# The MLP's last hidden tile with upper part, lower part and ones in one: two matrix products in place of three

## The chip, the cores and the metric

The kernel runs on one core of a Trainium2 chip. The metric is the device time of one execution in microseconds (us), the median of several runs. A core has TensorE (PE, matrix products into PSUM), VectorE (DVE), ScalarE (ACT), GpSimd (POOL) and the queue SP, which here issues every DMA.

## The reference

Two branches work on the layer-normed input `xn` of 4 x 1024 tokens of width 256: full attention with 16 heads of width 16, and two layers of windowed attention, each followed by an MLP. The output is `x + s * silu(g)`, with `s` from the first branch and `g` from the second. The MLP is the part that is changed:

```python
HID = int(DIM * 4 * 2 / 3)          # 682
h = shift_token(x)
mu = h.mean(-1, keepdims=True)
var = h.var(-1, keepdims=True)
h = (h - mu) / jnp.sqrt(var + 1e-05) * lg + lb
h = h @ w1 + b1
a, g = jnp.split(h, 2, axis=-1)
h = a * jax.nn.gelu(g, approximate=False)
x = x + h @ w2 + b2
```

## The kernel before

**Phases.** The second branch goes through phases: attention of layer 0 (phase 2), MLP of layer 0 (phase 3), attention of layer 1 (phase 4), MLP of layer 1 (phase 5). The 64 heads of the first branch (matrices `mx` and `sc`, exponentials `es`, sums `acc`; projections `pp`, `qa`, `th`) belong to no phase and are spread over the whole time, so that the two branches fill each other's gaps.

**The order** is not written by hand. A recorder takes down every operation with the tiles that it reads and writes. A list scheduler (`lay_out`) then gives each operation a price (`price`), lets each engine take what is due first (`nc.vt`), and so fixes one order for each engine; `put` issues the operations in that order (line 536 of the profile is there, so every operation has that line). Consecutive products into one PSUM bank are joined into pieces of up to 1500 ns of price. Each engine works through its queue in order.

**Precision.** Products with full precision are made from float32r parts: a value is split into an upper part (`split`: ACT copies with rounding) and a lower part (the rest, subtracted on VectorE or POOL), and `mm3` makes three products: upper x upper, upper x lower, lower x upper.

```python
def mm3(out, ah, al, bh, bl, start, stop):
    for k, (l, r) in enumerate(((ah, bh), (ah, bl), (al, bh))):
        nc.tensor.matmul(out, lhsT=l, rhs=r, start=start and k == 0, stop=stop and k == 2)
```

**The MLP** (`mlp_phase`) runs over 8 blocks of 512 tokens. The 682 hidden rows make 5 tiles of 128 rows and a sixth (`kt = 5`) of 42 (`TAIL`). For each block:

- `up` pieces (6 products of 128x512) make the gate half of the hidden rows; ACT adds the bias and puts them into `ge`, then one GELU goes over all six tiles. `ta` keeps the other half of the sixth tile.
- POOL clears rows 32 to 127 of the sixth tile of `ge` before that, and after the GELU sets rows 64 to 95 to 1. Row 64 is then the factor of `b2`, which the host has put into row 64 of the sixth tile of `w2`; the other rows meet zeros.
- VectorE multiplies: the sixth tile from `ta`, the others from PSUM as each `up` piece ends. Each tile is split into `hh` (ACT) and `hl` (POOL, 128x512 each).
- `y`: for each of four groups of 128 tokens, 6 tiles x 3 products of 128x256 into one bank, in pieces of 12 and 6; VectorE adds the residual (`xm`).
- In layer 1 SiLU, the output projection of the other branch (`foT`, `fth`, `ftl`, `fs`) and the last sum (`fx`) follow.

`ge`, `hh` and `hl` have one buffer each, so a block's first cast into `hh` waits until the block before has finished `y`. PSUM: three banks (`psB`) serve `up`, `y`, `dT` and other uses in rotation, two (`psM`) serve `mx` and `pp`, two `sc`, one `acc`.

**Weights.** `load_split` brings `w2` in by two DMAs and splits it into `w2_h` (ACT) and `w2_l` (POOL) at the start of each MLP phase.

Of the kernel before, what the change touches and what calls it, by code (L numbers as in the profile page):

```python
# [10 lines left out]
F32R = mybir.dt.float32r  # L11
# [3 lines left out]
ALU = mybir.AluOpType  # L15
# [4 lines left out]
P = 128  # L20
B, N, D = 4, 1024, 256
# [10 lines left out]
NKT = 6  # L32
TAIL = HID - 5 * P
W1T = 11 * P
BLK = 512
# [512 lines left out]
def f32(ap):  # L548
    return ap.bitcast(F32)
# [30 lines left out]
def fused_kernel(  # L580
# [17 lines left out]
    nc = Recorder(tc)  # L598
# [18 lines left out]
    def bank(name):  # L617
        return psB.tile([P, 512], F32, tag="b", name=name)
# [72 lines left out]
    def split(hi, lo, src, lo_eng=None):  # L691

        nc.scalar.copy(hi, src)
        (lo_eng or nc.vector).tensor_tensor(lo, src, f32(hi), ALU.subtract)
# [5 lines that stand above are left out]
# [219 lines left out]
    def stack(a):  # L919


        j, h = divmod(a, HALF)
        sq, sk = stacks[a % NSTACK]
        nc.vt = of_head(a - AHEAD - 1.0)
        at, m = 3 * DH * h, 3 * DH

        step = N // 2 if a < 2 else N
        for lo in range(0, N, step):
            s = slice(lo, lo + step)
            for g, dst in enumerate((sq, sk)):  # L930
                rows = qk_d[j % 2][g, at : at + m, s]
                three = rows.rearrange("(p s) t -> p s t", s=3)
                nc.sync.dma_start(dst[:m, s], rows)
                nc.sync.dma_start(dst[m : m + 2 * DH, s], three[:, g : g + 2, :])
                last = nc.sync.dma_start(dst[m + 2 * DH : 2 * m, s], three[:, 2 * g, :])
        if a >= NSTACK:
            last = nc.sync.dma_start(sq[96:98, :], sq[100:102, :])
        return last

    def maxima(a):  # L940

        sq, sk = stacks[a % NSTACK]
        nm = a2.tile([P, NC, 2], F32, tag="nm", name=f"nm{a}")
        for c in range(NC):
            nc.vt = of_head(a - AHEAD + c / NC)
            for n in range(2):
                ps = bank_a(f"mx{a}_{c}_{n}")
                nc.tensor.matmul(
                    ps, lhsT=sq[:, c * P : (c + 1) * P], rhs=sk[:, n * 512 : (n + 1) * 512],
                    start=True, stop=True,  # L950
                )
                nc.vector.tensor_reduce(nm[:, c, n : n + 1], ps, AX.X, ALU.max)
        mt = bank_t(f"mT{a}")
        mx = mt[:, 2 * P : 2 * P + NC]
        mp = mps[a % 2]
        nc.vector.tensor_reduce(mx, nm, AX.X, ALU.max, negate=True)
        nc.vector.tensor_copy(top(mp[:, 0, :]), mx)
        nc.vector.tensor_tensor(top(mp[:, 1, :]), mx, mp[:, 0, :], ALU.subtract)
        pt = mt[: 2 * NC, :P]
        nc.tensor.transpose(pt, mp.rearrange("p i c -> p (i c)"), ident)  # L960
        mr = a2.tile([2 * NC, P], BF16, tag="mr", name=f"mr{a}")
        nc.scalar.copy(mr, pt)
        for i in range(2):
            last = nc.sync.dma_start(
                sq[96 + i : 97 + i, :].rearrange("o (c t) -> o c t", t=P),
                mr[i * NC : (i + 1) * NC, :],
            )
        return last
# [63 lines left out]
    for a in range(-NSTACK, TOTAL):  # L1032
        m = a + NSTACK
        if a >= 0:
            attend(a)
        if m < TOTAL:
# [3 lines left out]
            last = stack(m)  # L1040
# [4 lines left out]
            last = maxima(m)  # L1045
# [6 lines left out]
    def load_split(pool, tag, hi, lo, src, name, lo_eng=None):  # L1052

        n = hi.shape[1]
        for i in range(0, n, 1024):
            m = min(1024, n - i)
            st = pool.tile([P, 1024], F32, tag=tag, name=f"{name}_{i}")
            nc.sync.dma_start(st[:, :m], src[:, i : i + m])
            split(hi[:, i : i + m], lo[:, i : i + m], st[:, :m], lo_eng or nc.gpsimd)
# [216 lines left out]
    def mlp_phase(layer):  # L1276
# [5 lines left out]
        p1 = nc.pool(f"m1_{layer}", 1, phase=nc.phase)  # L1282
# [13 lines left out]
        with nc.unit():  # L1296
            for t in range(11):
                m = P if t < 10 else 64 + TAIL
                for half in range(2):
                    nc.tensor.matmul(  # L1300
                        pb[:m, t : t + 1], lhsT=sts[half][:, t * P : t * P + m],
                        rhs=vec[:, 1, half : half + 1], start=(half == 0), stop=(half == 1),
                    )
        nc.vector.tensor_tensor(b1_sb[:, :10], b1_sb[:, :10], pb[:, :10], ALU.add)
        m = 64 + TAIL
# [6 lines left out]
        w2_h = wp.tile([P, NKT * D], F32R, name=f"w2h{layer}")  # L1312
        w2_l = wp.tile([P, NKT * D], F32R, name=f"w2l{layer}")
        load_split(p1, "ge", w2_h, w2_l, w2[layer], f"w2s{layer}")
        if layer == LAYERS - 1:
            wout_h = wp.tile([P, 2 * D], F32R, name="wouth")
            wout_l = wp.tile([P, 2 * D], F32R, name="woutl")
            load_split(p1, "ge", wout_h, wout_l, w_out, "wouts")
# [3 lines left out]
        for at, (b, i) in enumerate(blocks):  # L1322
            n = f"{layer}_{b}_{i}"
# [32 lines left out]
            def up(t):  # L1356
                ps = bank(f"up{n}_{t}")
                m = P if t < 10 else 64 + TAIL
                for half in range(2):
                    w = slice(t * P, t * P + m)  # L1360
                    mm3(ps[:m], w1_h[:, half, w], w1_l[:, half, w], dh[:, half], dl[:, half],
                        half == 0, half == 1)
                return ps
# [6 lines left out]
            ge = p1.tile([P, NKT, BLK], F32, tag="ge", name=f"ge{n}")  # L1370
            nc.gpsimd.memset(ge[32:64, 5, :], 0.0)
            nc.gpsimd.memset(ge[64:, 5, :], 0.0)
            for kt in (5, 0, 1, 2, 3, 4):
                ps = up(5 + kt)
                m, rows = (P, slice(0, P)) if kt < 5 else (TAIL, slice(64, 64 + TAIL))
# [7 lines left out]
            table(gelu)  # L1383
            nc.vt = of_layers(part, (at + 0.4) / len(blocks))
            hh = p1.tile([P, NKT, BLK], F32R, tag="hh", name=f"hh{n}")
            hl = p1.tile([P, NKT, BLK], F32R, tag="hl", name=f"hl{n}")
            for kt in (5, 0, 1, 2, 3, 4):
                m = P if kt < 5 else TAIL
                if kt == 5:

                    nc.gpsimd.memset(ge[64:96, kt, :], 1.0)
                    nc.vector.tensor_tensor(ge[:m, kt, :], ta[:m], ge[:m, kt, :], ALU.mult)
                else:
                    nc.vector.scalar_tensor_tensor(
                        ge[:, kt, :], up(kt), b1_sb[:, kt : kt + 1], ge[:, kt, :],
                        ALU.add, ALU.mult,
                    )
                split(hh[:, kt, :], hl[:, kt, :], ge[:, kt, :], nc.gpsimd)
            nc.vt = of_layers(part, (at + 0.7) / len(blocks))
            for k in range(4):  # L1400
                ps = bank(f"y{n}_{k}")[:, :D]
                for kt in range(NKT):
                    s, w = slice(k * P, (k + 1) * P), slice(kt * D, (kt + 1) * D)
                    mm3(ps, hh[:, kt, s], hl[:, kt, s], w2_h[:, w], w2_l[:, w], kt == 0, kt == NKT - 1)
                nc.vector.tensor_tensor(xr[:, k, :], ps, xr[:, k, :], ALU.add)
            if layer < LAYERS - 1:
                nc.sync.dma_start(
# [10 lines left out]
            for k in range(4):  # L1418
                pt = bank(f"foT{n}_{k}")[:, : 2 * P]
                for half in range(2):  # L1420
                    s = slice(half * P, (half + 1) * P)
# [4 lines left out]
                ps = bank(f"fs{n}_{k}")[:, :D]  # L1426
                for half in range(2):
                    s, w = slice(half * P, (half + 1) * P), slice(half * D, (half + 1) * D)
# [10 lines left out]
    for layer in range(LAYERS):  # L1439
        attention_phase(layer)  # L1440
        mlp_phase(layer)
# [91 lines left out]
```

## Time and profile before

| | |
|---|---|
| median of 3 runs | 2175.7 us (2174.28 to 2176.49) |
| profiled execution | 2178.46 us, its span 2176.7 us |
| mean granted TensorE clock | 0.987 |
| `y` products | 1152 of 128x256, 384 of each of three kinds, 154.8 us busy |
| `hl` splits on POOL | 96, median 1292 ns |
| `hh` casts on ACT | 96, median 620 ns |
| memsets of `ge` on POOL | 48, median 519 ns |
| layer 0's `y` | from 872.0 us |
| layer 1's `y` | to 2165.7 us |

The span runs from the first to the last instruction of the profiled execution; busy times are summed over one engine. Products on PE overlap, so the length of one `y` product (283 ns) is more than the distance to the next. The waits name what an engine stood for last; the chain is the one that ended last, followed back from the end.

### The profile page before, as it was taken

The numbers are of one execution on the slowest core, as the hardware profiler recorded it, in microseconds if no ns is written. First come the engines' busy times: TensorE is split into PE (matmuls) and PEld (weight loads), VectorE is DVE, ScalarE is ACT, GpSimd is POOL, SyncE is SP. The second block draws the span as 40 slices with busy tenths as digits, with TensorE's granted clock in tenths as the row PEclk, the third lists the DMA queues.
The fourth block names the chain that finished last, engine by engine and source line by source line (L and its number), as shares of the span: only waits on it lengthen the run. The fifth ranks groups of instructions, "written<-read, shape, count | busy, mean of one in ns | idle before, by whom it ended". The sixth has DMA issues, their size and how long they took to land.

```text
span 2176.7 us, 46620 instructions
## 1 busy us (share of the span) xinstructions
PE 2085.6 (96%) x16760; PEld 1376.1 (63%) x16760; DVE 1658.9 (76%) x4008; ACT 1604.4 (74%) x3830; POOL 1089.0 (50%) x1369
## 2 busy tenths in 40 slices
PE   4899999999999999999999999999999999999998
PEld 3356656666666645876665556666566665478887
DVE  6899799898888877576558888888888888855433
ACT  4577877788888777566658878778777788676774
POOL 5346755566666632333127556665657555023433
PEclk8799999999999999999999999999999999999999
DMA  4856655565565443231124535454354444503212
GB/s 129 169 118 162 157 129 119 136 153 112 115 126 131 95 109 101 78 83 60 35 84 116 131 77 102 105 126 101 69 112 108 89 90 86 153 11 97 77 50 83
DMA packets 496255, 227.62 MB, mean 105 GB/s; under 512 B 336788, under 2 KB 479264, under 8 KB 496024
## 3 DMA queue, kind: packets, MB, share of 16 engines
q1 hardware_dynamic: 496024, 224.63, 44.5%
q8 instruction: 133, 2.18, 0.4%
q14 instruction: 98, 0.80, 0.1%
HBM read 111.30 MB, written 49.82 MB: 74 GB/s over the span
## 4 chain that ended last, share of the span: by engine, by line
PE 64%; ACT 16%; DVE 9%; DMA 3%; issue 3%; POOL 2%; SPq 1%; ACTq 0%; POOLq 0%; DVEq 0%
PE up L536 11%; PE sc L536 7%; PE acc L536 7%; PE qkv L536 7%; PE mx L536 6%; PE y L536 6%; ACT sm L536 5%; PE po L536 5%; ACT es L536 3%; PE px L536 3%; PE sb L536 3%; DVE rotb L536 2%; DVE nm L536 2%; PE pp L536 2%; ACT ph L536 2%
## 5 line engine op out<-in xcount | busy, mean ns | idle before, releaser
L536 DVE TENSOR_REDUCE nm<-mx 128x1 f32<-128x512 f32 x1024 | 669.0, 682 | 106.2 <-PE mx L536 103.7
L536 ACT ACTIVATE es<-sc 128x512 f32<-128x512 f32 x1024 | 575.5, 600 | 151.3 <-PE sc L536 147.7
L536 PE MATMUL mx<-sk,sq 128*128 128x512 bf16 x1024 | 352.6, 387 | 22.1 <-DVE nm L536 15.6
L536 PE MATMUL sc<-sq,sk 128*128 128x512 bf16 x1024 | 343.7, 384 | 19.2 <-ACT es L536 15.8
L536 POOL TENSOR_TENSOR ph<-sm,ph 128x1024 f16<-128x1024 f32 (+1 forms) x128 | 258.6, 2021 | 177.9 <-ACT ph L536 163.3
L536 PE MATMUL qkv<-wqkvh,ht 128*128 128x512 f32 x768 | 302.0, 435 | 1.9 <-ACT sqv L536 0.5
L536 PE MATMUL acc<-es,v 128*32 128x512 f32 x2048 | 275.0, 609 | 0.3 <-ACT ac L536 0.2
L536 ACT ACTIVATE sm<-sm,nb 128x256 f32<-128x256 f32 (+1 forms) x512 | 247.4, 489 | 4.0
L536 POOL TENSOR_TENSOR qr<-rotb 128x256 f32<-128x256 f32 x256 | 182.9, 734 | 133.9 <-DVE rotb L536 120.3
L536 PEld LDWEIGHTS <-sq 128*128 128x128 bf16 x1024 | 89.9, 99 | 157.0 <-issue 112.3
L536 PEld LDWEIGHTS qkv<-wqkvh,ht 128*128 128x128 f32 x768 | 146.4, 191 | 57.4 <-ACT sqv L536 4.9
L536 PEld LDWEIGHTS <-pht 128*128 128x128 f16 x4800 | 151.5, 98 | 45.3 <-issue 30.2
L536 DVE TENSOR_TENSOR rotb<-qkv,tab 128x1024 f32<-128x1024 f32 x128 | 156.0, 1220 | 25.4 <-PE qkv L536 9.8
L536 PEld LDWEIGHTS <-sk 128*128 128x128 bf16 x1024 | 88.9, 98 | 130.3 <-issue 89.9
L536 POOL TENSOR_TENSOR hl<-ge,hh 128x512 fp32r<-128x512 f32 x96 | 122.2, 1291 | 96.5 <-ACT hh L536 95.5
L536 PE MATMUL po<-vs,pht 128*128 128x64 bf16 x4800 | 161.6, 193 | 2.8 <-DMA pht<-ph 2.2
L536 PE MATMUL qkv<-wqkvl,ht 128*128 128x512 f32 x384 | 152.1, 396 | 0.0
L536 PE MATMUL up<-dh,w1h 128*128 128x512 f32 (+1 forms) x352 | 148.5, 422 | 0.1
L536 POOL TENSOR_TENSOR sqv<-sqv 128x512 f32<-128x512 f32 (+1 forms) x128 | 129.6, 1013 | 37.6 <-ACT sqv L536 36.2
L536 PE MATMUL up<-dh,w1l 128*128 128x512 f32 (+1 forms) x352 | 139.1, 395 | 0.0
L536 PE MATMUL up<-dl,w1h 128*128 128x512 f32 (+1 forms) x352 | 138.8, 394 | 0.0
L536 ACT ACTIVATE sqv<-qkv 128x512 f32<-128x512 f32 x128 | 76.5, 597 | 70.5 <-DVE rotb L536 57.1
(271 smaller groups left out, 4739.1 us busy)
## 6 DMA issues: line engine op xcount, KB each, us to landing
xc<-xt_d SPq DMA_DIRECT2D x56, 256.0 KB
qk<-th SPq DMA_DIRECT2D x128, 96.0 KB
xt_d<-nt SPq DMA_DIRECT2D x32, 256.0 KB
ht<-xt_d SPq DMA_DIRECT2D x64, 128.0 KB
tab<-tab SPq DMA_DIRECT2D x64, 128.0 KB
xa<-xr SPq DMA_DIRECT2D x64, 128.0 KB
ht<-xa SPq DMA_DIRECT2D x32, 256.0 KB
xm<-xa SPq DMA_DIRECT2D x16, 512.0 KB
```

Source lines behind the costliest of these rows:

```text
L536: ins = getattr(getattr(nc, engine), method)(*[take(a) for a in args], **{n: take(a) for n, a in kw.items()})
```

## The change

In the sixth tile, 42 of 128 rows were in use, so upper and lower parts fit into one tile: `hh` holds the upper part in rows 0 to 41, the lower part in rows 64 to 105 and ones in rows 106 to 127. The host repeats the last 42 rows of `w2` from row 64 on and puts `b2` into rows 106 and 107. On the chip, after the split, row 107 of `w2_h` is overwritten with the lower part of `b2` by a one-row DMA, and rows 64 to 127 of the sixth tile of `w2_l` are cleared. One product with `w2_h` then gives upper x upper, lower x upper and both parts of the bias; one with `w2_l` gives upper x lower. `hl` has five tiles. The lower part of the sixth tile is subtracted on VectorE (42x512) instead of on POOL; the memset of `ge` after the GELU goes, and two memsets of `hh` (32x512) come.

```diff
@@ load of w2 in mlp_phase
         load_split(p1, "ge", w2_h, w2_l, w2[layer], f"w2s{layer}")
+
+        last = slice((NKT - 1) * D, NKT * D)
+        nc.sync.dma_start(f32(w2_h)[64 + TAIL + 1 : 64 + TAIL + 2, last], f32(w2_l)[64 + TAIL + 1 : 64 + TAIL + 2, last])
+        nc.gpsimd.memset(f32(w2_l)[64:, last], 0.0)
@@ a block
             hh = p1.tile([P, NKT, BLK], F32R, tag="hh", name=f"hh{n}")
-            hl = p1.tile([P, NKT, BLK], F32R, tag="hl", name=f"hl{n}")
+            hl = p1.tile([P, NKT - 1, BLK], F32R, tag="hl", name=f"hl{n}")
             for kt in (5, 0, 1, 2, 3, 4):
                 m = P if kt < 5 else TAIL
                 if kt == 5:
 
-                    nc.gpsimd.memset(ge[64:96, kt, :], 1.0)
+                    nc.gpsimd.memset(f32(hh)[32:64, kt, :], 0.0)
+                    nc.gpsimd.memset(f32(hh)[96:, kt, :], 1.0)
                     nc.vector.tensor_tensor(ge[:m, kt, :], ta[:m], ge[:m, kt, :], ALU.mult)
+                    nc.scalar.copy(hh[:m, kt, :], ge[:m, kt, :])
+                    nc.vector.tensor_tensor(
+                        hh[64 : 64 + m, kt, :], ge[:m, kt, :], f32(hh)[:m, kt, :], ALU.subtract
+                    )
+                    continue
                 else:
...
             for k in range(4):
                 ps = bank(f"y{n}_{k}")[:, :D]
-                for kt in range(NKT):
-                    s, w = slice(k * P, (k + 1) * P), slice(kt * D, (kt + 1) * D)
-                    mm3(ps, hh[:, kt, s], hl[:, kt, s], w2_h[:, w], w2_l[:, w], kt == 0, kt == NKT - 1)
+                s = slice(k * P, (k + 1) * P)
+                for kt in range(NKT - 1):
+                    w = slice(kt * D, (kt + 1) * D)
+                    mm3(ps, hh[:, kt, s], hl[:, kt, s], w2_h[:, w], w2_l[:, w], kt == 0, False)
+                for w2_x in (w2_h, w2_l):
+                    nc.tensor.matmul(ps, lhsT=hh[:, 5, s], rhs=w2_x[:, last], start=False, stop=w2_x is w2_l)
                 nc.vector.tensor_tensor(xr[:, k, :], ps, xr[:, k, :], ALU.add)
@@ on the host
-    w2[:, 5 * P + 64] = a["L0_ffn_b2"]
+    w2[:, 5 * P + 64 : 5 * P + 64 + TAIL] = a["L0_ffn_w2"][:, 5 * P :]
+    for k in range(2):
+        w2[:, 5 * P + 64 + TAIL + k] = a["L0_ffn_b2"]
```

As `lay_out` sees other prices and dependencies, it also gives every engine a slightly different order within the two MLP phases.

## The prediction

> **What bounds the kernel now.** I read the page first, for the engines' shares and the chain that ended last.
>
> ```profile
> PE 2085.6 (96%) x16760; PEld 1376.1 (63%) x16760; DVE 1658.9 (76%) x4008; ACT 1604.4 (74%) x3830; POOL 1089.0 (50%) x1369
> ...
> PE 64%; ACT 16%; DVE 9%; DMA 3%; issue 3%; POOL 2%; SPq 1%; ACTq 0%; POOLq 0%; DVEq 0%
> PE up L536 11%; PE sc L536 7%; PE acc L536 7%; PE qkv L536 7%; PE mx L536 6%; PE y L536 6%; ACT sm L536 5%; PE po L536 5%; ACT es L536 3%; PE px L536 3%; PE sb L536 3%; DVE rotb L536 2%; DVE nm L536 2%; PE pp L536 2%; ACT ph L536 2%
> ```
>
> TensorE (PE) is busy 96% of the span and makes 64% of the chain; `y`, the product that is changed, makes 6% of it. As busy time is an average over stages, I asked next for the windows of the two MLP phases and of the attention layer between them, for all work and then for `y` alone.
>
> ```profile
> 850.00:1136.00 286.00, 284.92 (x1640) 205.33 (x1639) 169.65 (x373) 178.16 (x286) 88.44 (x101) 1.00 0.21 59
> 1136.00:1905.00 769.00, 746.28 (x6697) 464.41 (x6696) 644.70 (x1544) 605.61 (x1577) 437.46 (x552) 1.00 0.47 106
> 1905.00:2177.00 272.00, 262.76 (x1603) 213.68 (x1601) 121.88 (x297) 183.86 (x266) 97.96 (x109) 0.99 0.21 64
> ```
>
> The columns are length, busy PE, weight loads, DVE, ACT, POOL, granted clock. In the first MLP phase PE idles 1.1 us of 286, in the second 9.2 of 272, at full clock; VectorE, ACT and POOL are at most 68% busy there (weight loads run under the products). What PE is spared in these stages should come off the end, unless a wait takes its place. Then the chain in order of time, for the pace of `y`, and the waits of PE:
>
> ```profile
> 882.82 5.76 PE y L536 x48
> ...
> 2041.64 5.75 PE y L536 x48
> ```
>
> ```profile
> PE y L536 <- POOL hl L536: 0.5, 1, 0.5
> ```
>
> 48 products in 5.75 us are 0.120 us each. (The 0.28 us that the `y` rows show is the length of one that overlaps the next.) The wait says that PE stood for `hl` once, 0.5 us, in the whole execution.
>
> **The change part by part.** *Products removed.* Each of 16 blocks has four groups of 128 tokens; each loses one of 18 products: 16 x 4 = 64. In the changed program's order of instructions `y` from `w2h` and `hl` falls from 384 to 320, and nothing else on PE changes in number. 64 x 0.120 = 7.7 us, in stretches where PE is the bound. What stands next to them changes little: PE's order is the same up to the first MLP phase and between the two; within them heads and MLP pieces swap neighbours.
>
> *POOL.* 16 `hl` splits go (1.29 us each by the `hl` row, 20.6 us) and 16 memsets of `ge` (0.52 us); 32 memsets of `hh` of the same form come. That frees 16 x (1.29 - 0.52) = 12.3 us of an engine that is half idle. PE waited 0.5 us for `hl`, so at most 0.5 us of it can be gained. The removed memset waited for the GELU; the new ones wait until the block before has read `hh`, its last `y`. In the block at 1950 us the GELU ended at 1949.6 and ACT's first `hh` cast stood for `y` until 1952.6, so POOL is released 3 us later. Behind it stand this block's `hl` (whose source waited for the same `y` anyway) and in the first phase some `th` and `qa` for heads that run later. In the second phase POOL is busy 98 of 272 us, so this is hidden. The sixth tile's cast on ACT must follow the memset by 0.52 us; PE has five `up` pieces of 1.4 us (7 us) to do before it needs `hh`. Without that cover it is 16 x 0.52 = 8.3 us. In the last block this cast now stands behind SiLU and its two table loads, ahead of the casts that `hl` wait for: one cast pitch, 0.5 us, near the end, where little is left to hide it. I count 0.5.
>
> *VectorE.* 16 subtractions of 42x512 come in. The nearest row is `ge<-ta,ge`, 42x512 with both inputs in SBUF: 0.68 us, so 10.9 us on an engine that is busy 59% and 45% in these phases. Each waits for the ACT cast, and VectorE's queue stands behind it: evictions of `up`, maxima of the heads. In five blocks of the second phase it is placed after the fourth of five evictions and in two after the third, by when the cast is due by the trace; in four of the eight blocks of the first phase it is placed ahead of the first eviction. Can it be lengthened? Two rows (shortest, median and longest, in ns) say what can happen to such an instruction:
>
> ```profile
> L536 DVE TENSOR_TENSOR tab<-tab,scl x16: 407/422/1397, 39.1 to 1272.0; 128x256 f32<-128x256 f32 x16
> ```
>
> ```profile
> L536 DVE TENSOR_TENSOR ge<-ta,ge x16: 673/682/684, 863.0 to 2140.6; 42x512 f32<-42x512 f32 x16
> ```
>
> `tab<-tab,scl` has both inputs in SBUF, as the new subtraction has; its median is 0.42 us and its longest 1.40. `ge<-ta,ge` never grew, but the POOL instruction beside it was a memset. The subtraction will stand among `hl` splits of 1.29 us. So one costs VectorE from 0.68 to 0.68 + 1.29 = 1.97 us. Does PE see it? An `up` piece takes 1.4 us and three banks are in rotation, so a bank may be evicted 2 x 1.4 = 2.8 us after its piece has ended; 1.97 + 0.75 for the eviction itself is 2.72. That is just covered, so I take nothing for it, nearest to the waits of PE on VectorE in the second phase (1.5 us in all); its other end is the first rival. The Trainium skill (SBUF — State Buffer, Who interferes with whom) says that a VectorE instruction with two SBUF inputs and a GpSimd instruction that reads SBUF exclude each other for the whole instruction, while one that only writes does not disturb; by that rule each subtraction may wait out a whole split, and the rival below is what it would do here. The trace agrees as far as it goes: `tab` grew by up to 0.98 us, and `ge<-ta,ge` beside memsets by nothing.
>
> *Setup.* Twice a one-row copy from `w2l` to `w2h` on SP and a 64x256 memset on POOL behind it. The nearest SP row, the two-row copies `sq<-sq`, takes 0.66 us to issue. In the first phase SP then stood 22 us at its loads of `xc` anyway; in the second the load of `wouts` is behind it, whose split on POOL began 6 us after the split of `w2` ended. `y` begins 24 and 42 us after that split. Nothing; uncovered some 3 us each. The first `hh` memset of a phase waits for the attention layer to let its space go; POOL idled 15.8 and 35.5 us there. Nothing.
>
> Sum: -7.7 + 0.5 = -7.2 us. Against the profiled execution (2178.46 us with a span of 2176.7) that is 2171.3; it lies 2.8 us above the median of 2175.7, from which 2168.5 follows.
>
> **The rivals.** *VectorE is held (slower).* In the first phase the subtraction waits out a split, or for a late cast, with `up` evictions and the heads' maxima (two banks only) behind it, and PE runs out of banks. Price at its full size: 8 x 1.97 = 15.8 us, so 2175.7 - 7.7 + 15.8 = 2183.8. It decides from 0.96 us a block in these eight (0.48 if all sixteen show it). For: the long `tab` rows; the placement ahead of the first eviction. Against: the waits of that phase list none of PE on VectorE (its weight loads waited 1.3 us, twice, on `ge`), and the sum of 2.72 against 2.8. In all sixteen it would be 31.5 us, the upper bound of the unknown price.
>
> *The first phase's half is lost.* There PE's work is a mix of heads and MLP; if heads become late by what the MLP gains (their loads on SP come no sooner), the 32 products spared there (3.8 us) turn into idle time, and 2175.7 - 3.8 = 2171.9. Against: PE idles 1.1 us in that phase and nearly every wait for PE is by others.
>
> *The new neighbours are worse.* If the first phase came to the idle share that the attention layer has, (769.00 - 746.28) / 769 = 3%, 8.4 us would be lost: 2175.7 - 7.7 + 8.4 = 2176.4. For: PE's order within the phases has changed in some 600 rows. Against: most are one piece exchanged with the next.
>
> **How the numbers follow.** The forecast, 2168.5, gets 0.70. It would lie between 2164.5 (the 0.5 us of `hl` gained, none lost in the tail, a run as far below its median as the lowest was here, 1.4 us, and some of the 9.2 us of idle time) and 2171.3. The lost half gets 0.10, the worse neighbours 0.08 (0.05 of it within, 0.03 above), the held VectorE 0.12. About 0.2%, 4.4 us, is what a measurement of this kernel can tell from no change: below 2171.3 is faster, above 2180.1 slower. So faster 0.70, same 0.15, slower 0.15. The range goes from 2164.5 to 2178: it takes in the lost half, the worse neighbours and the smaller sizes of a held VectorE.
>
> **What would show it.** Right: `y` from `w2h` and `hl` x320, PE busy down by about 8 us, idle time in both MLP phases as before, the second phase beginning about 4 us earlier. Wrong: new waits of PE on VectorE (`up` or `mx` behind the `hh` subtraction), a subtraction with a median far above 0.68 us, waits of `hh` on POOL's memset that reach PE, or a start of the second phase that has not moved.

## The result and the profile after

The changed kernel takes 2170.95 us in the median of 17 runs (2168.58 to 2173.74), beside 2176.06 us (2172.6 to 2179.85) for the kernel before on the same chip: a ratio of 0.9976 (95% interval 0.9968 to 0.9983), 5.2 us less, from 3.7 to 7.0. The forecast was 7.2 us less. The profiled execution took 2172.32 us, its span is 2170.4 us.

The page, engines and chain, in the lines that were shown of before:

```profile
PE 2069.0 (95%) x16578; PEld 1372.3 (63%) x16696; DVE 1671.5 (77%) x4024; ACT 1602.4 (74%) x3830; POOL 1078.5 (50%) x1371
...
PE 61%; ACT 17%; DVE 11%; issue 3%; DMA 3%; POOL 3%; SPq 1%; ACTq 0%; POOLq 0%; DVEq 0%
```

PEld, the weight loads, fell from 16760 to 16696, the 64 products. PE's own count fell by 182: 118 records of PE are missing in this profile, 88 of `mx` and 30 of `sc`. So PE's busy time can't be subtracted between the two pages, and I compare by the moments at which work begins and ends. DVE has 16 instructions and 12.6 us more, POOL 10.5 us less.

The two MLP phases (length, PE, weight loads, DVE, ACT, POOL, granted clock, DMA share, GB/s):

```profile
846.00:1130.00 284.00, 281.69 (x1603) 202.21 (x1614) 179.24 (x386) 178.81 (x289) 83.33 (x103) 1.00 0.21 60
...
1899.00:2170.40 271.40, 260.30 (x1567) 210.52 (x1571) 128.23 (x310) 183.31 (x266) 92.70 (x108) 1.00 0.21 65
```

PE idles 2.3 and 11.1 us (1.1 and 9.2 before); a few missing records are part of that (11 and 4 fewer than weight loads). The chain has the same two runs of `y`, now of 46 products, 5.51 and 5.52 us long, so still 0.120 us each:

```profile
881.47 5.51 PE y L536 x46
...
2036.55 5.52 PE y L536 x46
```

The wait of PE on `hl` has doubled, and no wait of PE on VectorE's `ge` or `hh` has come. Only its weight loads for `up` stand for `ge` a little more: five times, 2.1 us, in the first MLP phase, where it was twice, 1.3 us, before.

```profile
PE y L536 <- POOL hl L536: 1.0, 1, 1.0
```

The operations of the sixth tile (shortest, median, longest in ns; first and last start), and below them what the engines of `hh` stood for:

```profile
L536 PE MATMUL y<-w2h,hl x320: 274/283/388, 871.1 to 2159.3; 128*128 128x256 f32 x160
```

```profile
L536 POOL TENSOR_TENSOR hl<-ge,hh x80: 1263/1287/1743, 864.6 to 2151.7; 128x512 fp32r<-128x512 f32 x80
L536 POOL MEMSET hh<- x32: 516/518/523, 806.4 to 2138.7; 32x512 f32 x32
L536 DVE TENSOR_TENSOR hh<-ge,hh x16: 685/686/1592, 864.2 to 2143.4; 42x512 fp32r<-42x512 f32 x16
...
  PE y L536: 209.8, 12
```

`y` from `w2h` and `hl` is at 320 as forecast, and the subtraction's median is 0.69 us; but its longest is 1.59 us. POOL stands 209.8 us for the last `y` before its fills of `hh`.

A finer measure than the span is used below. Each MLP phase begins on PE with `pb`, 44 products of one column that make a bias. The work ahead of the first MLP phase is the same in all kernels, yet its end, the start of layer 0's `pb`, lies anywhere from 815.3 to 818.9 us in their profiles. So I count from there: to layer 1's `pb` (first MLP phase and second attention layer) and from that to the end (second MLP phase). Before, 1052.2 and 306.4 us; after, 1048.6 and 304.7. Layer 0 gave 3.6 us, layer 1 only 1.7. These are single profiles: two stretches that hold no change, e3's first and e2's second, differ from before by 0.5 and 1.3 us.

| kernel | median us | ratio to before, 95% interval | `pb` 0 to `pb` 1 | `pb` 1 to end |
|---|---|---|---|---|
| before | 2176.06 | | 1052.2 | 306.4 |
| changed | 2170.95 | 0.9976 (0.9968 to 0.9983) | 1048.6 | 304.7 |
| e1 third product, planned | 2186.8 | 1.0035 (1.0022 to 1.0048) | 1053.4 | 311.1 |
| e2 layer 0 only | 2176.39 | 0.9987 (0.9978 to 0.9996) | 1049.2 | 305.1 |
| e3 layer 1 only | 2176.39 | 0.9993 (0.9984 to 1.0002) | 1051.7 | 305.4 |
| e4 own tile | 2175.43 | 0.9989 (0.9980 to 0.9997) | 1047.8 | 308.7 |
| e5 third product, same order | 2178.33 | 1.0008 (0.9998 to 1.0018) | 1052.5 | 307.9 |
| e6 two products, e1's order | 2175.48 | 1.0000 (0.9992 to 1.0009) | 1050.2 | 309.3 |
| e7 subtraction twice | 2185.11 | 1.0044 (1.0032 to 1.0057) | 1051.7 | 316.1 |
| e8 own tile, two `fx` | 2168.22 | 0.9966 (0.9953 to 0.9979) | 1047.3 | 303.3 |
| e9 no subtraction | 2170.11 | 0.9959 (0.9945 to 0.9972) | 1049.2 | 303.7 |
| e10 two `fx` | 2176.38 | 0.9992 (0.9983 to 1.0001) | 1048.4 | 309.5 |
| e11 subtraction on POOL | 2172.41 | 0.9973 (0.9962 to 0.9984) | 1048.3 | 305.7 |
| e12 own tile, on POOL | 2172.24 | 0.9968 (0.9957 to 0.9980) | 1045.6 | 305.3 |

e1 to e4, e5 to e8 and e9 to e12 ran on three chips, 5 to 12 runs each, and each group shared its runs of the kernel before, whose medians there were 2178.2, 2175.38 and 2178.77 us; so ratios are compared, not medians. A ratio becomes microseconds by 2176.

### The profile page after: what moved, and what is told of

The parts are those of the page before. It is cut to its first block, busy times and chain, and to the rows that moved or that the text cites. A ratio compares the mean times of both kernels' runs of the same rounds, so it can differ in the third digit from the quotient of the medians.

```text
span 2170.4 us, 46388 instructions
## 1 busy us (share of the span) xinstructions
PE 2069.0 (95%) x16578; PEld 1372.3 (63%) x16696; DVE 1671.5 (77%) x4024; ACT 1602.4 (74%) x3830; POOL 1078.5 (50%) x1371
## 4 chain that ended last, share of the span: by engine, by line
PE 61%; ACT 17%; DVE 11%; issue 3%; DMA 3%; POOL 3%; SPq 1%; ACTq 0%; POOLq 0%; DVEq 0%
PE up L536 10%; PE acc L536 7%; PE sc L536 7%; PE qkv L536 7%; PE mx L536 6%; PE y L536 6%; ACT sm L536 5%; PE po L536 4%; ACT es L536 4%; PE px L536 3%; DVE nm L536 3%; PE sb L536 3%; DVE rotb L536 2%; ACT ph L536 2%; PE pp L536 2%
## 5 line engine op out<-in xcount | busy, mean ns | idle before, releaser
L536 PE MATMUL mx<-sk,sq 128*128 128x512 bf16 x936 | 327.6, 388 | 28.1 <-DVE nm L536 16.7
L536 PE MATMUL sc<-sq,sk 128*128 128x512 bf16 x994 | 334.7, 383 | 20.3 <-ACT es L536 14.6
L536 POOL TENSOR_TENSOR hl<-ge,hh 128x512 fp32r<-128x512 f32 x80 | 102.7, 1301 | 81.6 <-ACT hh L536 81.0
L536 POOL MEMSET hh<- 32x512 f32 x32 | 16.6, 519 | 225.8 <-PE y L536 209.8
```

The lines of the kernel that those rows point to most:

```text
L536: ins = getattr(getattr(nc, engine), method)(*[take(a) for a in args], **{n: take(a) for n, a in kw.items()})
```

## The experiments

### What are the 64 products worth, and what the order? (e1, e5, e6)

e1 gives the changed kernel its third product back, against a tile of zeros, with the planner counting it.

```diff
+        none = wp.tile([P, D], F32R, name=f"none{layer}")
+        nc.gpsimd.memset(f32(none), 0.0)
...
-                for w2_x in (w2_h, w2_l):
+                for w2_x in (w2_h[:, last], w2_l[:, last], none):
```

> The changed kernel, with a third product in each group of the sixth tile, of the same shape, with a tile of zeros as weights: the 64 products are back, all else of the change stays. Theory A (the 64 products are worth their full 7.7 us and the rest of the change, the subtraction on VectorE, the memsets on POOL and the later cast at the end, costs about 2.5 us): 7.7 us more than the changed kernel, so about 2178.6, 2.5 us above the kernel before. Theory B (the rest costs nothing, the products are worth only the 5.1 us measured): 5 us more than the changed kernel, within 1 us of the kernel before. Theory C (the gain came from the relief of POOL): stays near 2171, 5 us below the kernel before.

It is 1.0035 of before, so 12.8 us slower than the changed kernel by the ratios (0.0059): more than 64 x 0.120 = 7.7, and more than any of the three theories allowed. Since the third product's price also made `lay_out` write another order, two counterparts part the two causes. e5 issues the third product and hides it from the planner; e6 prices three and issues two.

```diff
 e5:
+                    op = nc.tensor.matmul(...)
+                op.calls.append(("tensor", "matmul", (ps,), dict(lhsT=hh[:, 5, s], rhs=w2_l[:, last], ...)))
 e6:
+                op.cost += D / 2.4 + 17.0
```

> The changed kernel with a third product of the sixth tile again (the second one issued twice, so the lower parts of W2 count twice in that tile), but given to the planner as free, so that every engine's order stays exactly the changed kernel's. Theory (all 64 products lie on the path at 0.120 us each): changed kernel + 7.7 us, that is 1.0011 of before (+2.5 us). Rival (part of the cut only lengthened waits that other work sets): changed kernel + 4 to 5 us, the same as before or below it (0.9990 to 1.0000). Rival (the cut was worth more than its matmuls, as the 12.8 us between the first experiment and the changed kernel would say): changed kernel + 11 us or more, 1.003.

> The counterpart: the changed kernel's two products in the order that the planner wrote when it counted three (the sixth tile's products are priced as three, 64 matmuls fewer are issued; the order on every engine is that of the first experiment, which took 1.0035 of before). Theory (0.120 us per product on any order; the rest of the first experiment's loss is its order): 7.7 us below the first experiment, 0.9999 to 1.0000 of before, and so some 5 us slower than the changed kernel with the very same instructions. Rival (the loss of the first experiment lies in the third product itself): as fast as the changed kernel, 0.9976.

With the orders kept, the 64 products are worth 1.0008 - 0.9976 = 0.0032, 7.0 us, on the changed kernel's order, and 1.0035 - 1.0000 = 0.0035, 7.6 us, on e1's; by the intervals each is good to some 3 us. By the profiles from the first `pb` on, e5 is 7.1 us longer than the changed kernel (1360.4 against 1353.3). e1 is only 5.0 us longer than e6 by theirs (1364.5 against 1359.5), but the execution of e1 that was profiled was the fastest of its five, 3.7 us below their median. So they lie on the path, nearly in full, as the theories of e5 and e6 had it. The order is the rest of e1's loss: e6 issues the very instructions of the changed kernel in another order and takes 0.0024, 5.2 us, more. By the profiles it is 6.2 us, 1.6 ahead of layer 1's `pb` and 4.6 behind it.

e5 also answers what the rest of the change costs, as it has as many products as the kernel before: 1.0008, so +1.7 us (-0.4 to +3.9), and 1360.4 - 1358.6 = +1.8 by the profiles.

### Does it work in each layer? (e2, e3)

```diff
+        new = layer in (0,)          # e3: (1,)
...
-                for w2_x in (w2_h, w2_l):
+                for w2_x in (w2_h, w2_l) if new else ():
```

> The change in the MLP of layer 0 alone; layer 1 as before. Forecast's own sum: 32 products, 3.8 us below the kernel before (about 2172.2). Theory 'VectorE is held in the first phase' (the stretched subtractions were seen there: 2.6 us each in two blocks): less than half of the whole gain, 1 to 2 us. If the first phase's half is lost: 0.

> The change in the MLP of layer 1 alone; layer 0 as before. Forecast's own sum: 3.8 us from 32 products less 0.5 at the end, 3.3 us below the kernel before (2172.8). The two traces put only 1.7 us of the 6.3 us of span here, so theory 'the shortfall is in the second phase' expects 1.5 to 2.

-2.8 us in layer 0 (from -0.9 to -4.8) and -1.5 in layer 1 (from -3.5 to +0.4), together -4.3 beside the whole change's -5.2. e2 lies between the forecast's 3.8 and the 1 to 2 of the held VectorE and can't part them; the "2.6 us" in its expectation are 1.01 us of waiting and 1.58 of subtraction. In the profiles the stretch that has the change gains 3.0 and 1.0 us (1052.2 to 1049.2, 306.4 to 305.4). Layer 1 gives less in both readings, though each interval is wider than the difference, and readings of 1 us don't bear much: e2's second stretch, which has no change, is 1.3 us shorter than before too, with a granted clock of 0.96 in the 46 us behind `pb` where before has 0.93.

### What does the subtraction cost? (e7, e9, e11)

e7 issues VectorE's subtraction twice, hidden from the planner; e9 puts a fill of zeros by VectorE in its place on the same order; e11 gives it to POOL, on an order of its own.

```diff
 e7:
+                    op.calls.append(op.calls[-1])
 e9:
+                    op.calls[:] = [("vector", "memset", (f32(hh)[64 : 64 + m, kt, :], 0.0), {})]
 e11:
-                    nc.vector.tensor_tensor(
+                    nc.gpsimd.tensor_tensor(
```

> The changed kernel with the subtraction of the sixth tile issued twice in a row on VectorE, given to the planner once, so that every order stays the changed kernel's. 16 more of 0.69 to 1.59 us on VectorE, 11 to 14 us. Theory (it lies beside PE's work, and only a few wait behind it): changed kernel + 0 to 1.5 us, 0.9976 to 0.9983 of before. Rival (VectorE held: each second of it reaches PE, as the rival of the prediction had it): + 11 to 14 us, 1.003 to 1.004. If the one subtraction costs the 2 us that the result lies short of the forecast, doubling it should cost about 2 us more, 0.9985.

> The changed kernel, every engine's order kept, with a fill of zeros by VectorE in place of each subtraction (42x512, no input read): the lower part of the sixth tile is left out of the result. The doubled subtraction cost 14.9 us, so the question is what the single one costs. Theory A (the single one is just covered, the doubled one ran past the cover): as the changed kernel, 0.9974 to 0.9978 of before. Theory B (the single one is what the result lies short of the forecast by): 2 us less, 0.9967. Theory C (each microsecond of VectorE reaches PE in these phases): at half the length, some 7 us less, 0.9944 or below.

> The changed kernel with the sixth tile's subtraction on POOL, where the kernel before had it (16 of about 1.3 us, the planner's order written anew, planned 3.4 us longer). Theory (VectorE has little cover left, but POOL's splits are what the last y waits for, and POOL has the two fills as well): 1 to 4 us slower than the changed kernel, 0.998 to 0.9995. Rival (the subtraction on VectorE costs the 2 us missing from the forecast): 2 us faster, 0.9967.

Doubling it is dear: 0.0068, 14.8 us, and 14.5 by the profiles, 11.4 of them in layer 1. My theory for that run fell, and its rival (11 to 14 us) came close. The groups of VectorE (busy us, mean ns, idle before) show why it is more than 16 x 0.69: the pairs took 33.8 us, 19.8 more than the single ones' 14.0.

```profile
L536 DVE TENSOR_TENSOR hh<-ge,hh 42x512 fp32r<-42x512 f32 x32 | 33.8, 1055 | 6.6 <-ACT hh L536 3.8 <-POOL hh L536 2.0
```

Waits of PE that e7 has and the changed kernel has not:

```profile
PE foT L536 <- DVE ge L536: 5.7, 4, 1.5
...
PE fs L536 <- DVE ge L536: 2.4, 2, 1.8
...
PE dT L536 <- DVE ge L536: 2.0, 3, 1.1
...
PE up L536 <- DVE ge L536: 1.3, 3, 0.5
```

They sum to 11.4 us, only 1.3 of them ahead of `up`. The timeline of one of them, VectorE and then PE (start, length, and in brackets the idle time before and who ended it):

```profile
1992.84 2.38 DVE L536 TENSOR_TENSOR hh<-ge,hh 42x512 fp32r<-42x512 f32 x2 [0.36 <-ACT hh L536]
1995.24 0.75 DVE L536 SCALAR_TENSOR_TENSOR ge<-up,b,ge 128x512 f32<-128x512 f32 x1
```

```profile
1996.05 0.77 PE L536 MATMUL foT<-ident,fo 128*128 128x128 f32 x4 [1.55 <-DVE ge L536]
```

The pair starts when ACT's cast is done and takes 2.38 us; the eviction of the last `up` piece stands behind it until 1995.24 and gives its bank back at 1995.99. PE has done two pieces of `fs` in the other two banks since 1992.92, 1.4 us; `foT`, the next, needs the third bank and has stood 1.55 us. The same place in the changed kernel:

```profile
1985.85 0.69 DVE L536 TENSOR_TENSOR hh<-ge,hh 42x512 fp32r<-42x512 f32 x1 [0.36 <-ACT hh L536]
1986.57 0.75 DVE L536 SCALAR_TENSOR_TENSOR ge<-up,b,ge 128x512 f32<-128x512 f32 x1
```

```profile
1987.38 0.77 PE L536 MATMUL foT<-ident,fo 128*128 128x128 f32 x4
```

Here the eviction ends at 1987.32, and `foT` begins at 1987.38 without a wait, behind two pieces of `fs` begun at 1985.94. So what covers the eviction of this block's last `up` piece is two pieces of `fs`, 1.4 us, and the single subtraction fits with 0.06 us to spare. The blocks at 1954 and 2018 us look the same.

The single one is another matter. e9's fill takes 0.485 us, so VectorE is spared 14.0 - 7.8 = 6.2 us, and the longest `hl` goes back from 1743 to 1308 ns. By the ratios e9 is 3.7 us faster than the changed kernel, with an uncertainty about as large; its interval (0.9945 to 0.9972) leaves out the values of theory A (nothing), holds that of B (2 us) and leaves out C (7 us) by a hair. By the profile from the first `pb` on it is only 0.4 us faster, but the execution profiled was the slowest of its five, 3.5 us above their median. e11 took the subtraction off VectorE altogether, on an order of its own and with more work for POOL, and is where the changed kernel is, 0.9973: both its theory and its rival missed. On this evidence a single subtraction costs anything from nothing to a few microseconds in all; that stays open, and POOL is no worse a place for it.

### A tile of its own (e4, e8, e10, e12)

The fills of `hh` wait for the last `y` of the block before. e4 puts the sixth tile into two tiles that last for the phase, filled once, taken in turn.

```diff
+        for k in range(2):
+            tails.append(wp.tile([P, BLK], F32R, name=f"h5{'ab'[k]}{layer}"))
+            nc.gpsimd.memset(f32(tails[k])[32:64], 0.0)
+            nc.gpsimd.memset(f32(tails[k])[96:], 1.0)
```

> The changed kernel with the sixth tile of hh as two tiles of their own in turn, whose zeros and ones are set once a phase: 32 memsets become 8, and neither POOL nor ACT waits for the last y of the block before to write the sixth tile. Theory A with the memsets as its cost: 1 to 2.5 us below the changed kernel (2168.5 to 2170). If the memsets and their waits cost nothing: within 0.7 us of the changed kernel, apart from what a new order does.

It came out 0.0013, 2.8 us, slower than the changed kernel, with intervals that overlap; neither expectation had it slower. Its last `y` began at 2153.0 us against 2159.5, and yet its end is later. Its chain at the end, in order of time, says where that went:

```profile
2159.78 1.46 POOL fx L536 x2
...
2161.25 2.91 DMA out<-fx
...
2164.18 3.98 DMA fx<-in_x
...
2168.40 0.72 POOL fx L536
```

The last block's `fx` is loaded into the one buffer of that name only when the block before has stored its own, and the order had put that block's last sums behind the last `y`. e8 gives `fx` two buffers, e10 does so in the changed kernel alone, and e12 is e8 with the subtraction on POOL.

```diff
-            xt = p1.tile([P, 4, D], F32, tag="fx", name=f"fx{n}")
+            xt = p1.tile([P, 4, D], F32, tag="fx", name=f"fx{n}", bufs=2)
```

> The fourth experiment (the sixth tile in two tiles of its own, filled once per phase; 0.9989 of before) with two buffers for fx, the tile that the last sum is made in. In that experiment the last y ended 6 us earlier than in the changed kernel and the end was lost at the tail: the last block's fx was loaded only after the block before had stored its own (2.91 us store, 3.98 us load, 2.76 us of sums behind it). Theory: with the wait on that store gone, some 7 us of it come back: 0.9955 to 0.9965 of before, 2 to 4 us faster than the changed kernel. Rival (the tail is held by SiLU and the products of fs behind it): nothing moves, 0.9985 to 0.9990.

> The changed kernel with nothing but the second buffer for fx: what of the gain of the eighth run is the buffer's. In the changed kernel the last sums on fx wait for no load, so theory: as the changed kernel (0.9974 to 0.9980), and the eighth run's 0.9966 is the own tiles' part with the end repaired. Rival (the buffer alone brings it): 0.9966.

> The eighth run (own tiles filled once, two buffers for fx; 0.9966) with the subtraction on POOL, which the fills no longer hold. Its plan is as long as the eighth run's. Theory (VectorE's cover is what is thin, as the doubled subtraction showed): 0 to 3 us faster than the eighth run, 0.9952 to 0.9966. Rival (POOL's 1.3 us ahead of the five other splits delays hl and so y): 2 to 4 us slower, 0.9975 to 0.9985.

e8 gives 0.9966, faster than before by 7.4 us and within 0.0001 of its theory. Its last sums on POOL wait for VectorE, no longer for a load:

```profile
2158.41 1.41 POOL L536 TENSOR_TENSOR fx<-fx,xm 128x256 f32<-128x256 f32 x2 [8.32 <-DVE xm L536]
2161.34 1.43 POOL L536 TENSOR_TENSOR fx<-fx,xm 128x256 f32<-128x256 f32 x2 [1.52 <-DVE xm L536]
```

From the start of the last `y` product it takes 10.7 us to the end (2156.0 to 2166.7), where e4 took 22.1. So the wait for the load is gone; but the order is another too, and the last `y` comes 6.0 us later after layer 1's `pb` than in e4, so 5.4 us remain of the 11.4. e8 is 2.2 us ahead of the changed kernel by the ratios, the best version here, but the intervals overlap; in the profile it is 2.7 us ahead, with a granted clock of 0.96 in the 46 us from layer 1's `pb` on where the changed kernel has 0.93, which by 46 x 0.03 explains some 1.4 of them. e12 is as fast as e8 within the intervals: again the runs show no difference between the two engines for the subtraction.

e10 missed both its values: 3.5 us slower than the changed kernel by the ratios (the intervals just touch), though nothing but a buffer was added. By the profile its loss is 4.8 us in the stretch from layer 1's `pb` on, all of it ahead of the first `y` there (69.0 us after `pb`, 64.2 in the changed kernel). Its first `up` comes 45.6 us after `pb`, in the changed kernel 39.7, and in these 46 us its granted clock was lower:

```profile
1865.00:1911.00 46.00, 41.62 (x215) 19.10 (x216) 40.38 (x131) 28.35 (x64) 6.24 (x7) 0.85 0.41 120
```

0.85 against 0.93 would be 3.7 us of 46. Whether the new order brings the low clock with it, one profile can't say.

## Why the prediction was right, and what was off

*Direction and products: right.* y's 64 products lie on the path. 7.7 us were forecast, 7.0 and 7.6 measured at kept order, each good to some 3 us. Of the signs named, `y` x320 and the earlier second phase came. PE's busy time can't be read for the missing records, and PE's idle time rose by 1.2 and 1.9 us in the two phases.

*The sum: 2 us too much.* Where the sum has -7.7 + 0.5 = -7.2, the products came out at -7.0 and all else at +1.7 (e5 against before, from -0.4 to +3.9); together that is the measured -5.2, as it must be with e5 in both. Both terms are within the error of these runs, the second less comfortably. The 0.5 itself is seen. In the last block the chain passes through two casts of `hh` on ACT ahead of `hl`, where it had one (start, length, count), here before and after:

```profile
2149.13 0.63 ACT hh L536
```

```profile
2142.39 1.16 ACT hh L536 x2
```

PE's wait for `hl` is 1.0 instead of 0.5 us. That a subtraction can lengthen a split was in no term: the first split behind these casts took 1.57 us, with the subtraction at 2143.41 beside it. What was mis-sized is the nothing for VectorE, setup and neighbours, about 1.7 - 0.5 = 1.2 us by e5. The profiles, as far as single ones go, put it into layer 1, where e5 needs 307.9 us for the stretch in which before needs 306.4: from `pb` to the first `y` 64.2 instead of 63.6 us, and between the first and the last `y` 232.8 instead of 231.9 with as many products, 0.5 of that being the wait for `hl`. No wait in the trace names the rest. "What stands next to them changes little" was taken at no price, and e6 and e10 show what such a price can be: 5.2 us for nothing but an order, and 3.5 for a buffer that leads to another order, with a lower clock beside it.

*Gain by layer.* "The second phase beginning about 4 us earlier" is right, layer 1's `pb` comes 4.6 us earlier, 3.6 of it since layer 0's. The second half of the sum, 3.3 us, was 1.7 by the profiles and 1.5 by e3, neither good to better than 1 us.

*POOL: right.* The fills of `hh` wait for `y` as told, 209.8 us in all, and PE doesn't see it. The "at most 0.5 us" that a shorter wait for `hl` could have given did not come, as that wait grew by the last block's 0.5.

*VectorE: the size was right, the cover was not.* The two ends of one subtraction, 0.68 and 1.97 us, hold the measured ones (0.69 to 1.59, mean 0.88). The sum "2.72 against 2.8" takes two `up` pieces as the cover. That fits the first phase, where the two longest (1.58 and 1.59 us) stood early in their blocks, with three evictions and their `up` pieces behind them. In five blocks of the second phase the eviction behind the subtraction is the block's last, and in three of them nothing but two pieces of `fs`, 1.4 us, covers it: 1.97 us would not have been covered there. It came out because the subtractions took 0.69 us there, with 0.06 us to spare in the block shown; as far as the sum goes, that was luck. With two, 2.38 + 0.75 = 3.13 us, the cover is gone, and e7 lost 14.8 us. The first rival was thus a real one, though for the other phase: 11.4 of e7's 14.5 us lie in layer 1, where the rival looked at the first phase. Whether the single subtraction costs nothing, as forecast, e9 leaves open.

*The other rivals.* By the profiles the first phase's half wasn't lost: 3.6 of 3.8 us came, 2.8 in e2. The worse neighbours didn't come to 8.4 us here; e6's 5.2 us show more than half of that to be possible.

*Two readings.* The second phase's `y` begins 31 us after the split of `w2` (1902.5 to 1933.9), not 42, and PE's waits on VectorE there are 1.9 us, not 1.5, with the 0.4 of `foT` on `xm`. Neither moves the sum.

## What to carry to other kernels

Where a planner writes the order, an edit's price has two parts, the instructions and the order that their prices lead to; issue an instruction that the planner isn't told of, or price one that isn't issued, and each can be measured alone. An operation that is just covered (by 0.06 us in the block shown) makes no wait and its double does, so a cover is worth stating as a sum of lengths beside a limit, for each place where the operation stands: the pieces that follow set the limit. Where a stage ends earlier and the end doesn't, look for a single-buffered tile in the tail.

## What the runs showed of the hardware

One of the long subtractions of the changed kernel, and POOL beside it, from the timelines of the two engines:

```profile
890.50 1.58 DVE L536 TENSOR_TENSOR hh<-ge,hh 42x512 fp32r<-42x512 f32 x1 [1.01 <-POOL hh L536]
```

```profile
890.25 1.29 POOL L536 TENSOR_TENSOR hl<-ge,hh 128x512 fp32r<-128x512 f32 x1
```

The split ends at 891.54, the subtraction at 892.08, 0.54 us later: it began beside the split and did most of its work after it. The one at 917.77 us shows the same (1.59 us, beside a split of 1.29 from 917.52), and 11 of the 16 took 0.69. The Trainium skill (SBUF — State Buffer, Who interferes with whom) states that a VectorE instruction with two SBUF inputs contends with a GpSimd instruction that reads SBUF, that the pair of ports the two share is an exclusive lock, and that a VectorE instruction with at most one SBUF input does not contend outside its two-port modes. These rows agree in the main: the longest subtraction is no longer than a split and one of its own length, and beside e9's fill, which reads nothing, no `hl` is longer than 1308 ns, where the changed kernel has 1743. The 0.54 us behind the split are 0.15 less than a subtraction takes alone; what it did in that time beside the split these rows don't say.

The granted clock of one stage differed between kernels (0.85, 0.93 and 0.96 in the 46 us behind layer 1's `pb`), which I had not expected. In slices of 4.3 us the changed kernel is low only in the two behind `pb`, 0.58 and 0.63 from 1867.9 to 1876.5 us. e10 is low there for longer, 0.50, 0.50 and 0.87 from 1867.9 to 1880.8, and again from 1889.4 to 1898.0, 0.72 and 0.89, where PE was busy only 2.40 of the first 4.30 us. Whether the order decides it or chance is open, with one profile of each.
